# Three edits of instruction order in a one-core graph-attention kernel: the 26 products of a score block, the sums of the projection, and the first column maximum

## The chip, the cores and the metric

The kernel runs on one core of a Trainium2 chip. The metric is the device time of one launch in microseconds (us). A core has TensorE (PE, matrix products, which write PSUM banks), VectorE (DVE), ScalarE (ACT), GpSimd (POOL) and SyncE (SP, which here only issues DMAs). Each engine works off its own list of instructions in order, and an instruction may wait on semaphores that others raise.

## The reference

Two layers over N = 3327 nodes with D = 512 features. Layer 0 holds two rounds of graph attention, which take nearly all the time:

```python
for l in range(2):                       # W_stack[l] is 512 x 1024
    Wh, Ws = split(x @ W_stack[l], 2)    # projection
    scores = Wh @ Ws.T                   # 3327 x 3327
    a = softmax(scores, axis=-1) * adj
    x = leaky_relu(a @ Wh + x, 0.01)
x = layernorm(x0 + x)
# layer 1: sign(x) @ sign(weight).T, then adj @ (.), relu, residual, layernorm
```

## The kernel before

All matrix work of the attention is fp32, and fast matrix-multiplication schemes save products. Rows of the score matrix are handled in 13 pairs of 128-row tiles (q, the keys and values side) against 13 pairs of columns (g, the queries side); seven chunks c of four tiles group the pairs two by two (the last chunk has one pair only).

**Projection** (`project`, once per round). For every chunk, PE makes seven products for each half of the queries ("one" and "two", line 627) and, woven between them, seven for each pair of values (line 562). The seven products share three PSUM banks: product 3 ends bank Y, from which DVE adds a block (line 222, `b` and `wb`); product 7 extends bank Z, from which DVE adds the block called c22 (line 222, `gsp` and `wh`), and product 4, the last, may only be added onto Z when that has been read. At the same time DVE does, for this and the next chunk, the "turns": the sums `gsp` and `ge` of the queries just made (lines 244, 375), the transposes `xT` of the next chunk's rows (line 278), its key sums `s` and the sums `xt` of its right operand (line 244), and the sums `t` of the values. `weave` sorts several lists into one program order by a place between 0 and 1: an item of a plain list of n gets (i + 0.5) / n, and an item that is a pair carries its own place. POOL makes a further set of sums (`quad_sums`) and issues the stores. Sums live in a ring of slots, so that a sum may have to wait until the store of the slot's former owner has landed.

**Scores** (`scores`, `quad_scores`). The loop over steps v builds a list of (place, operation) for each step and sorts it by place. Work of a later step can be put in `early[v + n]`. In each round some blocks of four pairs, the quads (i = 1 to 4 in round 0, 1 to 3 in round 1), are made with 26 products (line 809) in the order of `ORDER`; 26 products take four steps, and product number n stands at (n + 0.5) / 6.5. They share three banks at a time. A product that goes to bank P, Q, R, S or T may start when the reader of the product before it in the same bank is done. A reader is an ACT copy (`keep_as`, line 815) 0.03 step after its product, a DVE addition (`out`, line 821) 0.082 step after it, or `seed`, an ACT copy back into bank Q (line 818). The other blocks use seven products (line 769) in banks Z, Y, X, with DVE additions at lines 905 and 911 and ACT copies at 891, 886, 915 and 919.

While chunk 0 is scored there are no attention products yet, so PE does the scores alone. From chunk 1 on, seven products of `values` (line 1100) are woven into each step, between the score products.

**Softmax**. The running maximum of each column (`maximum`, line 868) ends in `column_max`: fold and turn (lines 953 to 957), `across` (nine small operations, lines 964 to 969; on DVE for the first two pairs, copies on ACT for the others), `back` (line 974). For the first pair `spread` (ACT, line 1019) follows. Three steps before the values of a pair, DVE subtracts the maximum (`shift`, line 1024) and ACT takes the exponential (lines 1029, 1030); then DVE adds to the total (1035), masks (1040), counts (1063), and POOL sums (1053, 1073 to 1076).

Of the kernel before, what the change touches and what calls it, by code (L numbers as in the profile page):

```python
# [29 lines left out]

B11, T1, T2, B22, T3, B21, T4 = range(7)
QUADS = ((1, 2, 3, 4), (1, 2, 3))
ORDER = (11, 3, 8, 23, 16, 14, 12, 9, 22, 1, 20, 25, 4,
         13, 21, 7, 24, 6, 19, 15, 18, 5, 10, 17, 2, 0)
STAGED = ((11, 3, 23, 16, 12, 22, 9, 1, 25, 20, 8, 14, 4),
          (13, 7, 19, 6, 5, 18, 17, 15, 24, 10, 0, 21, 2))
EXTRA = (3, 23, 22, 9, 20, 21, 13, 7, 5, 2)
# [8 lines left out]
def kernel(  # L46
# [206 lines left out]
    def right_sums(b11, b12, b21, b22, t1, t2, t3, t4):  # L253
        return sums_by(
            nc.vector, (t1, b12, b11, ALU.subtract), (t2, b22, t1, ALU.subtract),
            (t3, b22, b12, ALU.subtract), (t4, b21, t2, ALU.subtract),
        )

    def run(todo):
        for do in todo:  # L260
# [202 lines left out]
    def project(l, pre):  # L463
# [36 lines left out]
        def transpose_x(c, a):  # L500
            turn_x(xTs[c], a, rows_of[c][a])
# [152 lines left out]
        chains, pairs_of, of_pair, more_of, rest = {}, {}, {}, {}, []  # L654

        def prepare(c):
            start, *chains[c] = queries(c, (ch_lane, ch_lane if c else acc_lane))
            return start
# [21 lines left out]
            weave(parts[0][1], parts[1][1], prepare(0))  # L680
            rest += parts[0][2] + parts[1][2]
        for c in range(NC):
            turns = list(rest)
            rest = more_of.pop(c, [])
            if c + 1 < NC:
                for a in range(len(tiles_of(c + 1))):
                    turns.append(lambda a=a: transpose_x(c + 1, a))
                transpose_x_begin(c + 1)
                pairs_of[c + 1] = [
                    project_values(c + 1, a, acc_lane)  # L690
                    for a in range(len(tiles_of(c + 1)) // 2)
                ]
                for part in pairs_of[c + 1]:
                    turns += part[0]
                turns += prepare(c + 1)
            if c + 2 < NC:
                load_x(c + 2)
            if c == 0:
                weave(*chains[c], turns)
            else:  # L700
                one, two = chains[c]
                pairs = pairs_of[c]
                quad, sums = [], []
                if c in QUADS[l]:
                    quad = quad_sums(l, c, of_pair[2 * c], of_pair[2 * c + 1])
                if len(pairs) == 2:
                    sums = [(0.53 + 0.09 * n, do) for n, do in enumerate(pairs[0][2])]
                rest = pairs[-1][2] + rest
                weave(one + two, sum((part[1] for part in pairs), []), turns, quad, sums)
# [11 lines left out]
    def attention(l, att):  # L721
# [6 lines left out]
        asum, ws, out_, early = {}, {}, {}, {}  # L728
# [45 lines left out]
        def quad_scores(c, i):  # L774

            mine = halves_of(c)
            w = len(mine) * P
            for q in (2 * i, 2 * i + 1):
                for g in mine:
                    sc[g, q] = slot([P, 2, HW], F32, f"s_{l}_{g}_{q}")  # L780
            lo, hi = mine[0], mine[-1]
            at = {}
            for e in range(4):
                q = 2 * i + e // 2
                at[f"c{e}0"] = sc[lo, q][:, e % 2, :w]
                at[f"c{e}1"] = sc[hi, q][:, e % 2, HW - w :]
            bank = {}

            def fresh(n):
                at[n] = att.tile([P, w], F32, tag=n, bufs=1, name=f"q{n}_{l}_{c}_{i}")  # L790
                return at[n]

            begins = {11: "P", 8: "Q", 3: "R", 24: "S", 10: "T", 17: "V"}
            joins = dict(zip(
                (23, 12, 1, 4, 7, 6, 18, 14, 22, 25, 21, 19, 5, 2, 16, 9, 20, 13, 15, 0),
                "PPPPPPPQQQQQQQRRRRST",
            ))

            def one(r):
                b = begins.get(r) or joins[r]  # L800
                if r in begins:
                    bank[b] = ps_ch.tile([P, w], F32, tag="ch", name=f"p{b}_{l}_{c}_{i}")
                if r in QUERY:
                    kind, k = QUERY[r]
                    right = query(c, kind)[:, k]
                else:
                    n = EXTRA.index(r)
                    right = query_extra(c, n // 2)[:, n % 2]
                nc.tensor.matmul(  # L809
                    bank[b], xs[c, i, f"x{r}"], right, start=r in begins, stop=True,  # L810
                    skip_group_check=True,
                )

            def keep_as(b, name):
                nc.scalar.copy(at[name] if name[0] == "c" else fresh(name), bank[b])  # L815

            def seed(b, name):
                nc.scalar.copy(bank[b], at[name])

            def out(name, b, other):  # L820
                nc.vector.tensor_tensor(at[name], bank[b], at[other], ALU.add)  # L821

            def more(name):
                nc.vector.tensor_tensor(at[name], at[name], at["u3"], ALU.add)

            place = {r: (n + 0.5) / 6.5 for n, r in enumerate(ORDER)}
            got = [(at_, lambda r=r: one(r)) for r, at_ in place.items()]
            for r, b, name in (
                (11, "P", "c10"), (8, "Q", "c21"), (23, "P", "c11"), (14, "Q", "c31"),
                (22, "Q", "u2"), (1, "P", "c30"), (25, "Q", "u3"), (20, "R", "c01"),  # L830
                (4, "P", "c20"), (13, "R", "c00"),
            ):
                got.append((place[r] + 0.03, lambda b=b, name=name: keep_as(b, name)))
            for r, b, name, other in (
                (16, "R", "c10", "c10"), (12, "P", "c31", "c31"), (9, "R", "c11", "c11"),
                (21, "Q", "c10", "c10"), (7, "P", "c00", "c00"), (24, "S", "u3", "u3"),
                (6, "P", "c01", "c01"), (5, "Q", "c01", "c01"), (15, "S", "c20", "c20"),
                (18, "P", "c21", "c21"), (2, "Q", "c11", "c11"), (10, "T", "c21", "c21"),
                (17, "V", "c30", "c30"), (0, "T", "c31", "c31"),
            ):  # L840
                got.append((
                    place[r] + 0.082, lambda name=name, b=b, other=other: out(name, b, other)
                ))
            got += [
                (place[21] + 0.09, lambda: seed("Q", "u2")),
                (place[6] + 0.05, lambda: more("c30")),
                (4.2, lambda: more("c00")),
            ]
            tops = [(g, q) for q in (2 * i, 2 * i + 1) for g in mine]
            for n, (g, q) in enumerate(tops):  # L850
                place_ = (4.75, 5.35, 5.75, 6.35)[n]
                got.append((place_, lambda g=g, q=q: maximum(g, q)))
            for at_, do in got:
                k = int(at_ // 1)
                early.setdefault(v + k, []).append((at_ - k, do))
# [14 lines left out]
        def scores(c, q, s):  # L870
# [50 lines left out]
            if s == 1:  # L921

                after.append((-0.05, lambda: maximum(mine[0], q)))
                if q == NQ - 1:

                    whole = column_max(mine[0])
                    if mine[0] == 0:
                        whole[2] = (0.97, whole[2][1])
                        early.setdefault(v + 2, []).append((-0.03, whole.pop()[1]))
                    after.extend(whole)  # L930
                    for i in mine[1:]:
                        for n, at, (_, do) in zip(
                            (2, 2, 3, 4), (0.68, 0.68, 0.97, 0.68), column_max(i)
                        ):
                            early.setdefault(v + n, []).append((at, do))
            if s == 0:
# [84 lines left out]
        def shift(g, q):  # L1021
            s = sc[g, q]
            at = beside[l][:, 0:1]
            nc.vector.tensor_tensor(s, s, at.to_broadcast([P, 2, HW]), ALU.subtract)  # L1024

        def exponential(g, q):
            if q == 0:
                total[g] = att.tile([P, 2, HW], F32, tag="total", name=f"total_{l}_{g}")
                nc.scalar.activation(total[g], sc[g, q], AF.Exp)
            nc.scalar.activation(sc[g, q], sc[g, q], AF.Exp)  # L1030
# [266 lines left out]
        for v in range(-LOOK - 4, len(steps)):  # L1297
# [24 lines left out]
                ]  # L1322
            if 0 <= v + 3 < len(steps):
                s3 = steps[v + 3]
                work += [(0.0, lambda: shift(*s3)), (0.12, lambda: exponential(*s3))]
                if s3[1] == NQ - 1 and s3[0] + 1 < NQ:
                    work.append((0.9, lambda: spread(s3[0] + 1)))
            if 0 <= v + 2 < len(steps):
# [359 lines left out]
```

## Time and profile before

| | |
|---|---|
| median of three runs | 2543.01 us (2541.51 to 2543.59) |
| the profiled execution, its own time | 2545.97 us |
| its span on the core | 2544.2 us |
| mean granted TensorE clock | 0.995 |
| PE, DVE, ACT, POOL busy | 98%, 80%, 33%, 57% |
| PE waits for DVE at line 821 (score blocks) | 14.6 us in 22 places |
| PE waits for DVE at line 222 (projection) | 11.2 us in 8 places |
| PE waits for DVE at line 911 (score blocks) | 8.0 us in 6 places |

The stages in us from the span's start: projection of round 0 up to 198, scores alone from there to 295, scores and values to 1233; projection of round 1 from there to 1406, scores alone to 1500, scores and values to 2437; then the last layer. A 128x256 fp32 product shows as two MATMUL records 0.216 us apart, so 0.432 us each. A row of the timeline gives start, duration, engine, line, operation, output and inputs, count, and in brackets the idle time of the engine before it with the engine that ended it. The page counts a wait of PE from the modelled end of the matmul before; the time that a wait costs, by the distance of starts over the usual 0.216 us, is about 0.17 us more.

### The profile page before, as it was taken

The page shows a single profiled execution, that of the slowest core. Times are in us where ns is not written, and L with a number is a line of the kernel's source. Part 1 is how long each engine was busy: PE and PEld are TensorE (multiplying, and loading weights), DVE is VectorE, ACT ScalarE, POOL GpSimd, SP SyncE. Part 2 cuts the span into 40 slices and gives each one's busy share as a digit, 9 for nine tenths or more (in the row PEclk, how much of TensorE's full clock was granted, in tenths as well). Part 3 has the DMA queues.
Part 4 walks back from the last instruction along what each step waited for, and adds up shares of the span by engine and source line. Part 5 has one row for each costly group of instructions (what it writes and reads, how often), then busy time and mean ns, then how long its engine had stood idle before and what let it go on. Part 6 is the DMA issues. An engine that isn't in the chain of part 4 may idle for free.

```text
span 2544.2 us, 39239 instructions
## 1 busy us (share of the span) xinstructions
PE 2490.9 (98%) x12056; PEld 2146.4 (84%) x12056; DVE 2046.2 (80%) x4097; ACT 841.5 (33%) x2094; POOL 1459.8 (57%) x2452
## 2 busy tenths in 40 slices
PE   9999999999999999999999999999999999999998
PEld 7887888888888888888878788888888888888886
DVE  6976787887878888778897778788787887878876
ACT  3323333333333243322232333332333323232234
POOL 3873456666666666545686345566555665555531
PEclk9999999999999999999999999999999999999999
DMA  6776767777677776897778676867868777688985
GB/s 197 267 284 225 268 218 267 250 252 268 228 269 248 254 258 232 271 316 266 237 254 298 237 272 230 277 239 261 273 225 276 247 266 260 229 281 287 315 277 175
DMA packets 313958, 652.17 MB, mean 256 GB/s; under 512 B 35373, under 2 KB 170661, under 8 KB 313742
## 3 DMA queue, kind: packets, MB, share of 16 engines
q1 hardware_dynamic: 279022, 539.75, 63.4%
q0 software_dynamic: 34720, 109.84, 11.5%
q8 instruction: 99, 1.62, 0.3%
q14 instruction: 117, 0.96, 0.1%
HBM read 539.15 MB, written 110.29 MB: 255 GB/s over the span
## 4 chain that ended last, share of the span: by engine, by line
PE 86%; DVE 8%; DMA 2%; issue 1%; POOL 1%; ACT 0%; SPq 0%; DVEq 0%; POOLq 0%; ACTq 0%
PE acc L1100 37%; PE pZ L769 10%; PE pP L809 6%; PE pQ L809 6%; PE pY L769 5%; PE pR L809 4%; PE agg L1416 3%; PE pX L769 2%; PE pZ_wh L562 2%; PE pZ_g L627 2%; PE pT L809 1%; PE pS L809 1%; PE pY_wh L562 1%; DVE s L821 1%; PE pm L455 1%
## 5 line engine op out<-in xcount | busy, mean ns | idle before, releaser
L1073 POOL TENSOR_TENSOR as<-s 128x128 f32<-128x128 f32 x338 | 204.6, 605 | 650.2 <-DVE s L1040 449.6
L1100 PE MATMUL acc<-ws,s 128*128 128x256 f32 x1352 | 402.3, 379 | 0.0
L1100 PE MATMUL acc<-ws,as 128*128 128x256 f32 x1352 | 376.4, 379 | 0.4 <-DMA ws<-ws_d 0.4
L1100 PE MATMUL acc<-wh,s 128*128 128x256 f32 x1352 | 376.3, 379 | 0.0
L1030 ACT ACTIVATE s<-s 128x512 f32<-128x512 f32 x338 | 213.3, 631 | 421.0 <-DVE s L1024 419.8
L1053 POOL TENSOR_TENSOR deg<-deg,adj 128x256 fp8e4<-128x256 fp8e4 x338 | 255.6, 756 | 55.3 <-DMA adj<-in_adjT_dram 40.5
L1100 PEld LDWEIGHTS acc<-ws,as 128*128 128x128 f32 x1352 | 249.4, 190 | 36.0 <-issue 3.3
L1100 PEld LDWEIGHTS acc<-wh,s 128*128 128x128 f32 x1352 | 250.6, 190 | 32.6
L1100 PEld LDWEIGHTS acc<-ws,s 128*128 128x128 f32 x1352 | 250.8, 190 | 30.8
L1035 DVE TENSOR_TENSOR total<-total,s 128x512 f32<-128x512 f32 x312 | 251.7, 807 | 0.0
L1040 DVE TENSOR_TENSOR s<-s,adj 128x512 f32<-128x512 f32 x338 | 241.3, 714 | 4.7 <-DMA adj<-in_adjT_dram 0.5
L1024 DVE TENSOR_TENSOR s<-s,beside 128x512 f32<-128x512 f32 x338 | 228.1, 675 | 16.2 <-ACT beside L1019 16.1
L868 DVE TENSOR_TENSOR top<-top,s 128x512 f32<-128x512 f32 x286 | 228.0, 799 | 16.1 <-ACT s L919 13.5
L769 PE MATMUL pZ<-ga,xs 128*128 128x256 f32 (+1 forms) x912 | 214.2, 359 | 9.0 <-DVE s L911 8.0
L1074 POOL TENSOR_TENSOR s<-s 128x128 f32<-128x128 f32 x338 | 199.8, 591 | 26.8
L1075 POOL TENSOR_TENSOR as<-s 128x128 f32<-128x128 f32 x338 | 189.9, 562 | 26.5
L1100 PE MATMUL acc<-wh,as 128*128 128x256 f32 x676 | 201.2, 379 | 0.0
L1076 POOL TENSOR_TENSOR as<-s,as 128x128 f32<-128x128 f32 x338 | 183.6, 543 | 26.4
L769 PEld LDWEIGHTS pZ<-ga,xs 128*128 128x128 f32 x912 | 165.1, 190 | 33.7 <-DVE s L911 10.4
L905 DVE TENSOR_TENSOR s<-pY,u 128x256 f32<-128x256 f32 (+1 forms) x84 | 33.8, 402 | 150.4 <-PE pY L769 138.2
L815 ACT COPY s<-pP 128x256 f32<-128x256 f32 (+1 forms) x196 | 70.2, 358 | 245.5 <-PE pP L809 197.5
L1100 PEld LDWEIGHTS acc<-wh,as 128*128 128x128 f32 x676 | 123.1, 190 | 19.1 <-issue 3.3
(266 smaller groups left out, 5086.7 us busy)
## 6 DMA issues: line engine op xcount, KB each, us to landing
ws<-ws_d SPq DMA_DIRECT2D x338, 512.0 KB
adj<-in_adjT_dram SPq DMA_DIRECT2D x351, 256.0 KB
xs<-xq_d SPq DMA_DIRECT2D x98, 832.0 KB
xs<-xs_d SPq DMA_DIRECT2D x84, 512.0 KB
xs<-xs_d SPq DMA_DIRECT2D x84, 384.0 KB
gs_d<-gsp POOLq DMA_DIRECT2D x84, 256.0 KB, 3.7
ge_d<-ge POOLq DMA_DIRECT2D x60, 256.0 KB, 3.2
ga<-gs_d SPq DMA_DIRECT2D x54, 256.0 KB
```

The source lines that it names most:

```text
L769: nc.tensor.matmul(ch[bank], xs[c, q, a][:, k], query(c, b)[:, k], start=(start and k == 0), stop=(k == 1), skip_group_check=True,)
L809: nc.tensor.matmul(bank[b], xs[c, i, f"x{r}"], right, start=r in begins, stop=True, skip_group_check=True,)
L868: nc.vector.tensor_tensor(top[i], top[i], t, ALU.max)
L1024: nc.vector.tensor_tensor(s, s, at.to_broadcast([P, 2, HW]), ALU.subtract)
L1030: nc.scalar.activation(sc[g, q], sc[g, q], AF.Exp)
L1035: nc.vector.tensor_tensor(total[g], total[g], sc[g, q], ALU.add)
L1040: nc.vector.tensor_tensor(s, s, adj[g, q], ALU.mult)
L1053: nc.gpsimd.tensor_tensor(deg[:, g], deg[:, g], adj[g, q][:, a], ALU.add, saturate=False)
L1073: nc.gpsimd.tensor_tensor(s3, a11, a21, ALU.subtract)
L1074: nc.gpsimd.tensor_tensor(a21, a21, a22, ALU.add)
L1075: nc.gpsimd.tensor_tensor(s2, a21, a11, ALU.subtract)
L1100: nc.tensor.matmul(acc[g][i // 2][:, i % 2], a[i], b[i], start=(q == 0 and i % 2 == 0), stop=(q == NQ - 1), skip_group_check=True,)
```

## The change

Three things move; no operation is added or taken away.

1. `ORDER`, the order of the 26 products of a quad, becomes another one. Readers move with their products. `more("c30")` is tied to product 15 in the place of product 6.
2. In `project` the turns get weights (0.5 for the sums of the chunk before and the key sums, 1.1 for a transpose, 0.7 for the sums `xt`), and `spaced` puts each at the middle of its weight's share of the total. Before, all turns lay at equal distances.
3. Of the first pair's column maximum, `across` and `back` go from places 0.97 of one step and -0.03 of the next to 0.16 and 0.17 of that next step, and the `shift` and exponential of the first step go from 0.0 and 0.12 to 0.19 and 0.31. For the second pair of each chunk `across` goes from 0.97 of the third step after to 0.2 of the fourth.

```diff
-ORDER = (11, 3, 8, 23, 16, 14, 12, 9, 22, 1, 20, 25, 4,
-         13, 21, 7, 24, 6, 19, 15, 18, 5, 10, 17, 2, 0)
+ORDER = (8, 11, 3, 14, 23, 16, 22, 12, 9, 25, 1, 20, 21,
+         4, 13, 7, 24, 19, 5, 15, 6, 2, 10, 18, 17, 0)
...
+    def spaced(todo):
+        ends = [0.0]
+        for w, _ in todo:
+            ends.append(ends[-1] + w)
+        return [
+            ((a + b) / 2 / ends[-1], do) for a, b, (_, do) in zip(ends, ends[1:], todo)
+        ]
+
+    def heavy(w, todo):
+        return [(w, do) for do in todo]
...
-            turns = list(rest)
+            turns = heavy(0.5, rest)
...
-                    turns.append(lambda a=a: transpose_x(c + 1, a))
+                    turns.append((1.1, lambda a=a: transpose_x(c + 1, a)))
...
-                    turns += part[0]
-                turns += prepare(c + 1)
+                    turns += heavy(0.5, part[0])
+                turns += heavy(0.7, prepare(c + 1))
+            turns = spaced(turns)
...
-                (place[6] + 0.05, lambda: more("c30")),
+                (place[15] + 0.05, lambda: more("c30")),
...
                     if mine[0] == 0:
-                        whole[2] = (0.97, whole[2][1])
-                        early.setdefault(v + 2, []).append((-0.03, whole.pop()[1]))
+                        early.setdefault(v + 2, []).extend(
+                            (at, whole.pop()[1]) for at in (0.17, 0.16)
+                        )
...
-                            (2, 2, 3, 4), (0.68, 0.68, 0.97, 0.68), column_max(i)
+                            (2, 2, 4, 4), (0.68, 0.68, 0.2, 0.68), column_max(i)
...
-                work += [(0.0, lambda: shift(*s3)), (0.12, lambda: exponential(*s3))]
+                at = 0.0 if any(s3) else 0.19
+                work += [(at, lambda: shift(*s3)), (at + 0.12, lambda: exponential(*s3))]
```

Per bank, the products of a quad keep their sequence. The distances, in products, that differ: 7 to 6 in bank P (2 before, 5 after), 4 to 7 in bank P (3 before, 2 after), 13 in bank R to 24, which starts bank S in the same place (3 before, 2 after), 21 to 19 in bank Q with the seed between (4 before, 5 after).

On DVE the projection's order changes so (chunk 3 of round 0): all four `gsp` sums and two `ge` sums now stand ahead of the first half's c22 addition, where only the first two `gsp` sums stood ahead of the Y addition; all ten `ge` sums and the first transpose stand ahead of the first sum `t`; and six key-sum operations in the place of five stand ahead of the second half's c22 addition. In round 0's chunk 4 and round 1's chunks 3 and 4 the number of key sums ahead of that addition stays six.

## The prediction

> **What bounds the kernel now.** I began with the page's first and fourth parts: which engine is busy, and of what the chain that ended last is made.
>
> ```profile
> PE 2490.9 (98%) x12056; PEld 2146.4 (84%) x12056; DVE 2046.2 (80%) x4097; ACT 841.5 (33%) x2094; POOL 1459.8 (57%) x2452
> ...
> PE 86%; DVE 8%; DMA 2%; issue 1%; POOL 1%; ACT 0%; SPq 0%; DVEq 0%; POOLq 0%; ACTq 0%
> ```
>
> PE sets the time; DVE's 8% of the chain are the moments at which PE waits for it. No product is added or removed, so only such moments can change. The view of the waits, for PE, says where:
>
> ```profile
> PE pP L809 <- DVE s L821: 14.6, 22, 2.0
> PE pZ_g L627 <- DVE gsp L222: 11.2, 8, 2.9
> PE pZ L769 <- DVE s L911: 8.0, 6, 2.5
> ```
>
> Columns: total, times, longest. I then read the timeline around the longest waits. The projection, PE and then DVE:
>
> ```profile
> 121.72 1.03 PE L562 MATMUL pX_wh<-wa,xT 128*128 128x256 f32 x4
> 125.64 2.07 PE L627 MATMUL pZ_g<-xt,m 128*128 128x256 f32 x4 [2.89 <-DVE gsp L222]
> 127.51 1.91 PE L562 MATMUL pZ_wh<-wsum,xT 128*128 128x256 f32 x4
> ```
> ```profile
> 106.45 0.42 DVE L222 TENSOR_TENSOR b<-pY_g,h_g 128x256 f32<-128x256 f32 x1 [0.29 <-PE pY_g L627]
> ...
> 115.36 0.57 DVE L244 TENSOR_TENSOR t<-wb,wh 128x256 f32<-128x256 f32 x1 [1.82 <-DMA gs_d<-gsp]
> ...
> 125.17 0.41 DVE L222 TENSOR_TENSOR gsp<-pZ_g,h_g 128x256 f32<-128x256 f32 x1
> ```
>
> Product 4 waits until DVE's c22 addition at 125.17 has read bank Z. DVE was 90% busy from 98 to 125 (24.22 of 27.00 us), yet stood idle 1.82 us at 115.36, because the first sum `t` needs a slot whose store had not landed. And four records of 1.03 us become four of 1.9 us: after the stall the granted clock is 0.50 (125.6 to 128.4) and 0.59 (128.4 to 132.4). So a stall can cost twice.
>
> The first column maximum:
>
> ```profile
> 282.92 0.45 DVE L974 STREAM_TRANSPOSE off<-mx 128x256 f32<-128x256 f32 x1
> 283.39 0.38 ACT L1019 COPY beside<-off 128x256 f32<-128x256 f32 x1 [2.85 <-DVE off L974]
> 283.80 0.69 DVE L1024 TENSOR_TENSOR s<-s,beside 128x512 f32<-128x512 f32 x1 [0.44 <-ACT beside L1019]
> 284.41 0.42 DVE L911 TENSOR_TENSOR s<-pZ,p 128x256 f32<-128x256 f32 x1
> 284.88 1.70 PE L769 MATMUL pZ<-ga,xs 128*128 128x256 f32 x4 [2.16 <-DVE s L911]
> 285.19 0.63 ACT L1030 ACTIVATE s<-s 128x512 f32<-128x512 f32 x1
> 286.62 0.37 ACT L919 COPY s<-pZ 128x256 f32<-128x256 f32 x1 [0.54 <-PE pZ L769]
> ```
>
> The addition of line 911 stands behind `across`, `back` and `shift`, PE behind it, and the clock is halved again. A quad while PE has scores alone:
>
> ```profile
> 253.39 0.95 DVE L868 TENSOR_TENSOR top<-top,s 128x512 f32<-128x512 f32 x1
> 254.26 0.41 DVE L821 TENSOR_TENSOR s<-pP,s 128x256 f32<-128x256 f32 x1
> 254.73 0.70 PE L809 MATMUL pP<-ga,xs 128*128 128x256 f32 x2 [0.85 <-DVE s L821]
> ```
>
> Product 6 follows 7 in bank P at two products' distance, and the reader of 7 stands behind a 0.95 us maximum. Costs below go by distances of starts over the usual pitch: this stall is 1.02.
>
> **Part 1, the projection.** Chunk ends now cost, in chunks 2, 3 and 4: round 0 1.96, 3.05 and 1.24 us, round 1 1.99, 3.09 and 0.41; 0.9 us more in three small ones (0.35, 0.39, 0.16). Behind each stall of 3 us, 14 records at 0.43 for 0.216 lose 2.9 to 3.0 more.
>
> DVE's idle time ahead of these additions, by the gaps in its timeline: round 0 chunk 2 1.13 + 0.44 + 0.72; chunk 3 0.7 + 1.8; round 1 chunk 2 1.14 + 0.44 + 0.75, chunk 3 2.3. After the change, `gsp` sums, `ge` sums and the first transpose stand there ahead of `t` and have their inputs, so they fill much of it; their own places later come free, and the c22 addition moves forward. Against that, one more key sum (a 0.41 to 0.53 us row, spaced 0.4) stands ahead of the second half's addition in chunk 3 of round 0. Chunk 3: 3.05 - 2.5 + 0.45 = 1.0 if only the second half gains nothing more; placing operations one by one with their durations I get 0.6, and 0.8, 0.1 for chunks 2 and 4. Round 1: 0.8, 0.7, and 1.0 for chunk 4, where DVE's 2.23 us idle at 1350.13 is a load that no order hastens. Stalls of 1.96, 1.99 and 2.15 us (98.31, 1306.53, 1699.84) left the clock alone, so both slow stretches go. Sum: round 0 -1.16 - 2.45 - 2.9 - 1.14 = -7.7; round 1 -1.19 - 2.39 - 3.0 + 0.6 = -6.0. I take 12 of the 13.7, since the transposes wait for loads that POOL and SP issue in their own order (`xT` waited for one until 1353.7). Ends: all stalls gone, 1.96 + 3.05 + 1.24 + 1.99 + 3.09 + 0.41 + 0.9 + 5.9 = 18.5 gained; no idle time filled and a key sum added in four chunks, 2 lost.
>
> **Part 2, the order of 26.** No instruction is added. Two regimes.
>
> c = 0, PE alone (seven quads, 0.43 us per product). Product 6 stalls now: 1.02 five times, 0.32 twice, 5.7 in all. At distance 5 this is gone. Late next is product 7, at distance 2 behind 4 instead of 3; and bank P was made free there by a copy, while bank Q's chain is longer: 21's DVE addition, ACT's `seed`, the next product's copy, all ahead of the copy of 4 on ACT. End of 21 to start of 7: 0.63 + 0.42 + 0.04 + 0.27 + 0.37 + 0.05 = 1.78, against 1.3 that three products give: 0.5 each. Product 20, behind a maximum in five quads: 0.3 each. So 7 x 0.5 + 5 x 0.3 = 5.0, net -0.7. The first quad's wait for its load (0.70 at 213.92, 1.36 at 1420.38) meets a product one place later: -0.43 twice. The bank R stall of 0.72 at 1443.33 likewise: -0.4. Together -2.0. Ends: -9 (no stall left in these quads) and +3 (0.43, one more product's time, seven times).
>
> c from 1 on (42 quads; `values` products lie between, 0.865 us per product). Product 6 stalls five times, all in round 1, i = 2 (0.66, 0.77, 0.77, 0.65, 1.85), where residual work and a maximum delay DVE. There product 7 stalls instead, its chain 0.2 longer, the worst one 0.75: 6.3 for 4.7, +1.6. Product 18 stalls six times (0.91, 0.33, 2.15, 1.23, 0.77, 0.62: 6.0); its predecessor's reader comes one product earlier relative to it, which leaves 2.15 - 0.865 = 1.3, 0.4 and 0.05, 1.9 with some rounding up: -4.1. In the other 37 quads I find 0.5 to 1.2 us between the seed chain's end and product 7, hence nothing. Net -2.5. Ends: -11 (all go) and +5 (a further 0.12 in each quad, a quarter of the 0.5 found at c = 0).
>
> **Part 3, the column maximum.** First pair: the addition of line 911 now runs at once, 281.90. `across` to `shift` took 283.80 - 281.43 = 2.37 us, and starts at 282.24: `shift` at 284.61. What queues behind this on ACT: `spread`, two exponentials, and then the copies of lines 915 and 919. The exponentials start at 285.33 and 285.98, the copies at 286.52 and 286.8, and the next block's product, whose bank the last copy reads, at 287.2. Without a stall it would start at 284.29 (284.88 - 2.32, plus four records of 0.43): 2.9 lost. Before, 2.32 and 2.67 (1491.49) were lost here, so +0.6 and +0.2. DVE lets PE go; ACT stops it.
>
> The clock: stalls of 3.05 and 3.09 cost 2.9 to 3.0 more, that of 2.32 cost 1.5 (seven records), that of 2.67 none (granted clock 1.00 from 1491 to 1494). 2.9 is nearest to the 3 us rows: 2.9 each, 5.8 less 1.5 = +4.3. Second pair: `across` out of the way at 0.2, the stalls of 1.41 at 294.12 and 1499.05 go: -2.8. Part 3: 0.8 + 4.3 - 2.8 = +2.3. Ends: -9.3 (all of it gone: 5.0 + 1.5 + 2.8) and +5.1 (second pair gains nothing).
>
> The Trainium skill's page "TensorE: Matmul & The Clock Gate", Part 1, speaks of a free-running window of 3413 ns in which PE must be idle before its clock is halved, and advises against idle gaps above about 3 us. By that alone no stall of 2.32 us should have halved anything, yet the trace shows it at 284.88; by the page part 3 would be 4.3 us cheaper and the time that much lower. The same page has ACT and DVE as strict FIFO: it speaks against this part, since copies of ACT that are ready cannot pass exponentials that are not.
>
> **Sum.** -12 - 2.0 - 2.5 + 2.3 = -14.2. The profiled execution took 2545.97 us, its span 2544.2 and 1.8 around it; 2545.97 - 14.2 = 2531.8. It lies 3.0 above the median of 2543.01, so I forecast 2528.8 us for the median.
>
> **Rivals.** A measurement of this kernel tells about 0.2%, 5.1 us, from no change.
>
> *The projection stays with DVE.* For: 90% busy there, and the `t` sums' slots still come free when stores land, up to 115.26 in chunk 3. Then stalls shrink by about 1 us each in four chunks, the 3 us ones stay above 2, and one of the slow stretches stays: -4 for -12, 2537.
>
> *Spacing does nothing at all.* `t` waits for the same store, and DVE idles elsewhere: +2 for -12, with the rest 2543, no change.
>
> *Slower: the seed chain.* Product 7 at distance 2 waits in every quad, not in five. It takes a 21 whose DVE addition is late by the 0.5 to 1.2 us of slack and more, for instance behind a maximum or a mask. Against: only round 1's i = 2 shows such lateness now. For: the new order shifts all readers. At 0.5 us per quad, 42 quads cost 21: 2550. From 14.2/42 = 0.34 us per quad on it outweighs all the gains.
>
> *Better: the new ACT wait is short.* If the first pair's stall stays under 2.2 us, the clock stays up: part 3 is -2.8 - 1.5 - 0.6 for +2.3, and with a projection at -13 the time is 2521.
>
> **How the numbers follow.** Forecast 0.45, by itself 2522 to 2536; better 0.18; projection half 0.15; nothing from spacing 0.08; seed chain 0.14. Range 2516 to 2543: it leaves out the seed chain and the far ends of the best case. Faster by over 5.1 us (below 2537.9): 0.45 + 0.18 + two thirds of 0.15 = 0.73; within: 0.05 + 0.08 = 0.13; slower 0.14.
>
> **What will show it.** PE's waits for `gsp` at line 222: from 11.2 us to about 4, no granted clock of 0.5 near 126 and 1334. Waits of PE at product 18 gone save two or three; product 6 replaced by product 7, with an ACT copy as releaser. At 284 to 288 PE waits for ACT's copy (line 919 before, 931 now), with halved clock behind it; at 294 and 1499 no wait. I am wrong if product 7 waits outside round 1's i = 2, if line 222's sum stays above 8, or if the first pair shows no ACT wait.

## The result and the profile after

The changed kernel is slower: 2555.25 us (2552.61 to 2556.02, five runs) against 2543.59 us, ratio 1.0045 with a 95% interval of 1.0031 to 1.0060. The forecast was 2528.8 us, range 2516 to 2543. The profiled execution took 2555.67 us, its span 2553.9; before it was 2545.97 and 2544.2.

The page, part 1 and the first line of part 4, of the kernel after:

```profile
PE 2491.3 (98%) x12056; PEld 2145.2 (84%) x12056; DVE 2051.6 (80%) x4097; ACT 833.4 (33%) x2094; POOL 1460.5 (57%) x2452
...
PE 35%; DVE 4%; issue 1%; ACT 1%; POOL 0%; DVEq 0%; ACTq 0%; POOLq 0%
```

PE works as long as before, so again only its waits have changed. (The chain of part 4 covers only 41% of the span this time, so its shares can't be set against those before.) The view of waits, PE's rows, of the kernel after (total, times, longest):

```profile
PE pP L821 <- ACT s L827: 23.3, 24, 1.8
PE pQ L821 <- DMA xs<-xq_d: 6.7, 5, 2.1
PE pZ_g L638 <- DVE gsp L222: 5.4, 9, 1.0
PE pY_g L638 <- ACT gsp L235: 4.2, 1, 4.2
PE pY L781 <- ACT s L931: 3.9, 2, 2.2
```

Read against the view before, the change did what it says: of the three DVE releasers only line 222 is left in the first rows. It fell from 11.2 to 5.4 us with none above 1.0; line 911 (923 now) left the first rows. But ACT, which released almost nothing before, now holds PE for 23.3 + 4.2 + 3.9 us, and a load for 6.7. Each stage taken from its first product on (before: 193.1, 295.1, 1233.0, 1400.6 and 1500.0 us), the time moved so (change of a stage's length in the two profiled executions, after minus before; the execution before had the clock halved behind both 3 us stalls of its projections and lay 2.4 us above its median):

| stage | round 0 | round 1 |
|---|---|---|
| projection | -5.3 | +2.6 |
| scores alone | +0.6 | -0.6 |
| scores and values | +4.7 | +8.1 |

So the loss lies mainly in "scores and values", where the forecast had -2.5 us, and the projection's gain in round 0 is half undone in round 1. Of 24 waits in the first row, twelve are of product 7. The other twelve are of product 23, once in each first quad (i = 1) of the chunks from 1 on: 0.89 to 1.94 us each by distances of starts, 16.6 us together. No step of the forecast speaks of product 23.

The timeline of the kernel after around one of them, ACT, DVE and PE rows picked out:

```profile
442.39 0.40 ACT L982 COPY mx<-mx 32x8 f32<-32x8 f32 x2
442.81 0.37 ACT L1139 COPY op<-acc 128x256 f32<-128x256 f32 x1
...
443.22 0.42 DVE L1140 TENSOR_TENSOR h<-acc,op 128x256 f32<-128x256 f32 x1 [1.07 <-ACT op L1139]
...
448.58 0.68 DVE L1037 TENSOR_TENSOR s<-s,beside 128x512 f32<-128x512 f32 x1
...
449.29 0.63 ACT L1043 ACTIVATE s<-s 128x512 f32<-128x512 f32 x1 [2.52 <-DVE s L1037]
449.83 0.35 ACT L827 COPY s<-pP 128x256 f32<-128x256 f32 x1
...
450.23 0.70 PE L821 MATMUL pP<-gb,xs 128*128 128x256 f32 x2 [0.91 <-ACT s L827]
```

The same place before, where the quad's first product starts at 450.20 (in the kernel after at 445.71):

```profile
446.09 0.37 ACT L1126 COPY op<-acc 128x256 f32<-128x256 f32 x1 [0.23 <-PE acc L1100]
446.49 0.42 DVE L1127 TENSOR_TENSOR h<-acc,op 128x256 f32<-128x256 f32 x1 [0.24 <-ACT op L1126]
...
450.89 0.37 ACT L815 COPY s<-pP 128x256 f32<-128x256 f32 x1 [1.41 <-PE pP L809]
...
451.95 0.68 DVE L1024 TENSOR_TENSOR s<-s,beside 128x512 f32<-128x512 f32 x1
...
452.66 0.63 ACT L1030 ACTIVATE s<-s 128x512 f32<-128x512 f32 x1 [1.40 <-DVE s L1024]
```

Two edits meet here. In the new `ORDER` product 11 is the second product and not the first, so its ACT copy (`s<-pP`) moved from place 0.11 to 0.26, past the exponential at 0.12: before it ran 1.77 us ahead of the exponential, now behind. And `across` of the second pair, at 0.2 of the fourth step, put its ACT copies (line 982) ahead of the copy `op` (ACT's copy of an attention product, which DVE adds to the output sum `h`): `op` starts 2.9 us ahead of the quad's first product in place of 4.1, DVE's `h` is late by as much, and so are the sums and the maximum behind it, `shift` (2.87 after the first product in place of 1.75) and the exponential. Product 11's copy waits for all of that, and product 23 for the copy.

### The profile page after: what moved, and what is told of

Its sections match the earlier page's. It is cut to its first block, busy times and chain, and to the rows that moved or that the text cites. A ratio compares the mean times of both kernels' runs of the same rounds, so it can differ in the third digit from the quotient of the medians.

```text
span 2553.9 us, 39256 instructions
## 1 busy us (share of the span) xinstructions
PE 2491.3 (98%) x12056; PEld 2145.2 (84%) x12056; DVE 2051.6 (80%) x4097; ACT 833.4 (33%) x2094; POOL 1460.5 (57%) x2452
## 5 line engine op out<-in xcount | busy, mean ns | idle before, releaser
L880 DVE TENSOR_TENSOR top<-top,s 128x512 f32<-128x512 f32 x286 | 233.7, 819 | 16.1 <-ACT s L931 13.5
L1087 POOL TENSOR_TENSOR s<-s 128x128 f32<-128x128 f32 x338 | 194.3, 575 | 26.8
L1069 POOL DMA_DIRECT2D adj_d<-ab x169 | 94.4, 559 | 62.7 <-ACT ab L1061 35.0
```

What stands on the lines that cost most here:

```text
L880: nc.vector.tensor_tensor(top[i], top[i], t, ALU.max)
L1087: nc.gpsimd.tensor_tensor(a21, a21, a22, ALU.add)
```

## The experiments

Times are medians; "before" was 2543.9 to 2544.8 us beside these runs. Ratios are to the kernel before with 95% intervals; differences to the changed kernel are to its 2555.25 us, taken beside a kernel before of 2543.59.

**e1, the order alone.** The diff's `ORDER` and `more("c30")`, applied to the kernel before.

> The kernel before with the new ORDER (and its more) alone. Theory: the order costs time because product 11, moved from the first to the second place, has its ACT copy behind the exponential at 0.12, so product 23 waits in each first quad of the chunks from 1 on (12 stalls, 16.6 us in the changed kernel), against about 5 us won at products 6 and 18: slower by 10 to 14 us, near 2555. Rival, the order is good and the loss lies in the projection and the column maximum: faster by 3 to 6 us, near 2539.

2545.29 us, ratio 1.0005 (0.9995 to 1.0014). Neither theory: alone, the order changes nothing that can be measured. Product 23's twelve stalls are six of 0.33 to 0.52 here. That the forecast's 4.5 us did not come is seen in the waits inside the quads, which (those over 0.25 us) add to 23.6 us by starts against 23.4 before: gone are those of products 6 (10.4), 18 (6.0) and 13 (2.4), and in their place stand product 7 with 11.6 (the forecast had 9.8), product 21 with 3.8, most of it for loads, product 23 with 2.3 and products 2 and 10 with 1.8. The forecast had no term for products 23, 2 and 10.

**e2, the spacing alone.** The weights, `spaced` and `heavy`, applied to the kernel before.

> The kernel before with the weights and spacing of the projection alone. Theory: round 0 gains 5 to 6 us; round 1 gives back what it gains at line 222 to one wait of 4.4 us of the ACT copy of c21 in chunk 4, whose ring slot now has another former owner, and to the halved clock behind it (2.7 us), net +3: near 2541, faster by 2 to 3 us. Rival, that stall comes from DMA traffic of this one execution: then it is missing here and the time is 2534, faster by 9 us.

2545.23 us, ratio 1.0005 (0.9995 to 1.0014). The wait for the slot (of `c21`, the block that ACT copies from bank Z after product 4) is there again (4.5 us), so it isn't of one execution; the gain expected over it did not show in the median.

**e3, the column maximum alone.** Both pairs' new places applied to the kernel before.

> The kernel before with the column maximum's new places alone. Theory (DVE lets PE go, ACT stops it): the stalls of 2.3 and 2.7 us at line 911's readers become stalls of about 2 us at the next block's product with halved clock in both rounds, the second pair's 1.4 us go twice: between 3 us faster and 1 us slower, near 2542.5. Rival, the ACT wait is new cost with nothing gained: 4 us slower or more.

2548.08 us, ratio 1.0016 (1.0007 to 1.0026): the rival's number, though not its reason. Its two halves are taken apart below (e15, e16).

**e4, the exponential behind the copy.**

```diff
-                work += [(at, lambda: shift(*s3)), (at + 0.12, lambda: exponential(*s3))]
+                till = 0.28 if c > 0 and i == 4 else at + 0.12
+                work += [(at, lambda: shift(*s3)), (till, lambda: exponential(*s3))]
```

> The changed kernel with the exponential of one step per chunk (the one in which the first quad starts, chunks 1 to 6) put at place 0.28 in the place of 0.12, just behind the ACT copy of product 11. Theory: the stalls of product 23 go, 12 of 1.06 to 1.94 us: faster than the changed kernel by 14 to 17 us, near 2540. Rival, the copy is late by itself (product 11 or bank P are late, or the exponential's delay moves the stall to the sums and masks behind it): less than 4 us gained, 2551 or more.

2541.23 us, 14.0 less than the changed kernel, ratio 0.9988 (0.9978 to 0.9998). All twelve stalls of product 23 are gone. Timeline of e4 at the same place (first product at 441.31):

```profile
442.86 0.37 ACT L827 COPY s<-pP 128x256 f32<-128x256 f32 x1 [0.49 <-PE pP L821]
...
444.77 0.59 PE L821 MATMUL pP<-gb,xs 128*128 128x256 f32 x2
...
444.89 0.63 ACT L1043 ACTIVATE s<-s 128x512 f32<-128x512 f32 x1 [1.66 <-DVE s L1037]
```

The copy runs 2 us ahead of the exponential, and product 23 (444.77) waits for nothing. The exponential itself lost no time: it starts 3.58 us after the first product, as in the changed kernel.

**e5, `across` put back.**

```diff
-                            (2, 2, 4, 4), (0.68, 0.68, 0.2, 0.68), column_max(i)
+                            (2, 2, 3, 4), (0.68, 0.68, 0.97, 0.68), column_max(i)
```

> The changed kernel with the second pair's across put back to 0.97 of the third step. Theory (two edits meet): across at 0.2 stands ahead of ACT's copy op, which holds DVE's output sums, maximum and shift 1.1 us later, and with them the exponential behind which product 11's copy waits; put back, the stalls of product 23 fall from 16.6 us to about 2.5, the two of 1.4 us at the second pair return: faster than the changed kernel by 10 to 13 us, near 2543. Rival, the order alone makes them: no more than 2 us gained, 2553 or more.

2543.7 us, 11.6 less than the changed kernel, ratio 1.0000 (0.9990 to 1.0009). Product 23's stalls are 2.6 us. With e1 and e3 this fills the square: order without `across` 2.3 to 2.6 us of stalls at 23, both 16.6, `across` without the new order none at 23. It takes both.

**e6, another owner for the slot.**

```diff
-            turns = spaced(turns)
+            turns = spaced([(1, do) for _, do in turns] if (l, c) == (1, 4) else turns)
```

> The changed kernel with equal weights in one chunk, the turns of chunk 4 of round 1. The ring then gives c21's tile of that chunk a slot whose former store was issued far earlier. Theory: the stall of 4.4 us and the halved clock behind it (2.7 us) go, a wait at line 222 of 0.4 to 2.3 us comes back: faster than the changed kernel by 4 to 7 us, near 2550. Rival, the stores of that time are late for whoever needs a slot, and DVE's or ACT's next owner stops PE as long: less than 2 us gained.

2553.12 us, 2.1 less than the changed kernel, which is not clear of noise (ratio 1.0042, 1.0027 to 1.0056, against 1.0045): the rival, as far as this can tell. The wait in the kernel after, and what took its place in e6 (timelines):

```profile
1352.44 0.37 ACT L235 COPY gsp<-pZ_g 128x256 f32<-128x256 f32 x1 [6.83 <-DMA ws_d<-t]
1352.87 2.07 PE L638 MATMUL pY_g<-xt,msum 128*128 128x256 f32 x4 [4.21 <-ACT gsp L235]
```
```profile
1351.76 0.37 ACT L219 COPY h_g<-pY_g 128x256 f32<-128x256 f32 x1 [5.93 <-DMA ws_d<-t]
1352.18 1.22 PE L638 MATMUL pY_g<-xT,msum 128*128 128x256 f32 x2 [3.30 <-ACT h_g L219]
```

c21's copy got a free slot; the next copy that needs one (`h_g`) stands before a store of the same kind. In both kernels ACT goes on at about 1352, when a `ws_d` store of `t` lands.

**e7, the first exponential behind ACT's copies.**

```diff
-                work += [(at, lambda: shift(*s3)), (at + 0.12, lambda: exponential(*s3))]
+                work += [(at, lambda: shift(*s3)), (0.12 if any(s3) else 0.72, lambda: exponential(*s3))]
```

> The changed kernel with the first step's exponential at 0.72 in the place of 0.31, behind ACT's copies of lines 927 and 931. Theory: the next block's product no longer waits for the copy (2.4 and 1.9 us) and the clock stays up (1.7 us each): faster than the changed kernel by 5 to 8 us, near 2548. Rival, the loads of that time are late too (0.4 and 1.0 us before the same products) and take the place of the wait, or a later wait for the exponential appears: less than 3 us gained.

2551.34 us, 3.9 less than the changed kernel, between theory and rival (ratio 1.0033, 1.0019 to 1.0047; the interval overlaps that of the changed kernel). The waits for the copy fell from 2.4 and 1.9 us (by starts) to 0.9 and none; a load and a second copy behind it took 0.4 to 1.3 us.

**e8, three repairs.** e4, e6 and e7 together, and `across` at 0.2 for the second pair of chunk 0 only (`if i == 1`).

> The changed kernel with the three repairs together: exponential at 0.28 in the step of the first quad, across at 0.2 for the second pair of chunk 0 only, equal weights in chunk 4 of round 1, first exponential at 0.72. Theory: the gains add, 14 + 6 + 6 off 2555: near 2529, faster than the kernel before by 12 to 16 us. Rival, the waits are replaced by others behind them: 2538 or more.

2535.49 us, ratio 0.9961 (0.9945 to 0.9977): faster than both kernels. It is 19.8 us below the changed kernel, and e4, e6 and e7 gained 14.0 + 2.1 + 3.9 = 20.0: the repairs seem to add up, and two of them were expected to be worth more. The fourth edit, `across`, was not run by itself on top of e4, so the sum takes it as worth nothing there.

**e9, the seed chain.**

```diff
-                (place[21] + 0.09, lambda: seed("Q", "u2")),
+                (place[4] + 0.04, lambda: seed("Q", "u2")),
```

> The changed kernel with the seed at 0.04 step behind product 4 in the place of 0.09 behind product 21, that is behind ACT's copy of 4 in the place of ahead of it. Theory (seed chain): product 7, at distance 2 behind 4, no longer waits for 21's DVE addition; its 12 stalls (3.9 us while PE has scores alone, 6.7 us in round 1, i = 2) go but for 1 to 2 us: faster than the changed kernel by 6 to 9 us, near 2548. Rival, distance 2 is too short by itself, or DVE's lateness stops the next product (24 or 19) instead: less than 4 us gained.

2555.86 us: nothing gained, the rival. PE's waits in e9:

```profile
PE pP L821 <- ACT s L827: 14.4, 12, 1.8
PE pQ L821 <- DMA xs<-xq_d: 8.4, 6, 3.1
PE pS L821 <- ACT s L827: 5.9, 7, 2.4
```

Product 7's twelve waits are gone (the twelve that are left are product 23's). But in round 1, i = 2, product 24 now waits, for the copy of 13, which now stands behind the late seed and an exponential: 6.4 us by starts for the 6.7 before. While PE has scores alone the 3.9 us at product 7 did go. What took them back is product 24 in the other quads: laid start by start against the kernel after, the two having one order of PE's products, product 7 wins 10.9 us over all 49 quads and product 24 loses 12.1, in places of 0.2 to 0.3 us besides those of i = 2. (This profiled execution, the slowest of the five at 2560.39, also has one wait for a load of 3.2 us at 1092.91 with the clock at 0.57 behind it.)

**e10, five repairs.** e8, the seed of e9, and in `STAGED` (which half of a quad's left operands is loaded first) products 21 and 4 exchanged, with ACT's copies of them in `quad_sums`.

> The three repairs with two more: the seed as in the run before, and product 21's left operand loaded with a quad's first half and product 4's with the second (the new ORDER starts 21 at place 12, where the load of the first half ended before). Theory: 7 us from product 7 and 2 to 4 us from product 21's waits for loads off 2535.5: near 2525, faster than the kernel before by 16 to 21 us. Rival, waits replaced by others: 2532 or more.

2531.65 us, ratio 0.9952 (0.9938 to 0.9966): 3.8 less than e8, not the 10 expected. No run takes its two additions apart; e9 gained nothing by the seed alone, while the waits of product 21 (7.8 us by starts in e8) became waits of 1.8 at product 4.

**e11, the repairs with the old order.** e8 with the old `ORDER` and `more`.

> The three repairs with the old ORDER. Theory: the new order without seed and load repairs is worth about 4 us (products 6, 18, 11 and 13 stall 22 us in the old one, 7, 20, 21 and 8 some 18 in the new): near 2538, slower than the three repairs with the new order by 1 to 5 us, and by 10 or more than the five repairs. Rival, the order is worth nothing or costs: 2534 or less.

2538.91 us, ratio 0.9981 (0.9972 to 0.9990): 3.4 more than e8 (all eleven runs lie above all five of e8) and 7.3 more than e10 (the intervals lie apart). With its collisions removed the new order pays.

**e12, spacing in round 0 only.** e10 with `spaced([(1, do) for _, do in turns] if l == 1 else turns)`.

> The five repairs with equal weights in all of round 1, spacing in round 0 only. Theory: in round 1 the slots' stores stop PE in one way or the other, so that the spacing there is worth 1 to 4 us only: near 2527, slower than the five repairs by that. Rival, spacing is worth as much as in round 0 (5 to 6 us), 2531 or more; or less than nothing there, 2524 or less.

2530.84 us, ratio 0.9953 (0.9939 to 0.9967): the fastest, not distinguishable from e10, which has equal weights in round 1's chunk 4 already. In the rest of round 1 the spacing is worth nothing that can be measured.

**e13 and e14, the spacing in one round each,** on the kernel before (equal weights where `l == 1`, then where `l == 0`).

> The kernel before with the spacing in round 0 only. Theory: round 0 wins the stalls at line 222 (about 4 us; the halved clock behind the 3 us stall is a matter of chance, so it adds 1 to 2 us on average and not 2.9): faster by 3 to 6 us, near 2540. Rival, the first quads then wait for loads that come no earlier and give it back: within 2 us of the kernel before.

> The kernel before with the spacing in round 1 only. Theory: the wait of ACT's copy for its slot (4.4 to 5 us, with halved clock at times) takes what line 222 gives: between 2 us faster and 3 us slower. Rival, round 1 is where spacing alone loses everything that round 0 wins: 4 us slower or more.

e13: 2540.83 us, ratio 0.9983 (0.9975 to 0.9992), 3.4 faster. e14: 2547.97 us, 1.0012 (1.0003 to 1.0021), 3.7 slower; its profile has the same wait for `gsp` at line 235, 4.2 us. Together they are e2: a gain in round 0, the same lost in round 1.

**e15 and e16, the halves of the column maximum,** on the kernel before: the second pair's `across` alone, then the first pair alone.

> The kernel before with the second pair's across at 0.2 of the fourth step alone. Theory: it takes the two stalls of 1.4 us (2.8 us) and holds DVE's output sums back by 1.1 us in each chunk from 1 on, where the product that fills beside then waits (0.3 to 1.0 us in 11 places): slower by 1 to 4 us, near 2546. Rival, without the new order there is enough slack in each chunk: 2 to 3 us faster.

> The kernel before with the first pair's edit alone. Theory: one wait for another, 1.2 to 1.9 us at the next product and 1.0 to 1.6 at a load for 2.3 to 2.7 at line 911: within 2 us of the kernel before. Rival, it is this half that costs the 4 us: 3 us slower or more.

e15: 2547.63 us, 1.0015 (1.0006 to 1.0024). e16: 2542.42 us, 0.9996 (0.9986 to 1.0005). e3's cost lies in `across`. In e15's profile "scores and values" is 2.9 and 3.5 us longer than before, and PE waits where it never did (e15, waits):

```profile
PE beside L1151 <- DVE s L1024: 1.6, 2, 0.8
...
PE pQ L809 <- ACT s L815: 0.7, 1, 0.7
```

The product that fills `beside` comes once per chunk, behind the late `shift`. The second row is product 14 of a first quad (1502.42), behind ACT's copy of product 8. So even without the new order the delay reaches PE. Laid start by start against the kernel before, `beside` accounts for 1.0 of the 2.9 us and 2.0 of the 3.5, product 14 for 0.8 and 2.2 (in e3: 1.0 and 2.0, 0.7 and 2.2); what is left in round 0 falls on products 9 and 11. No run isolates one of them.

## Why the prediction was wrong

Sum against measurement (medians, us):

| term | forecast | measured alone |
|---|---|---|
| projection | -12, from round 0 -7.7 and round 1 -6.0 | +1.2 (e2); round 0 -3.4, round 1 +3.7 (e13, e14) |
| order of 26 | -4.5 | +1.3 (e1) |
| column maximum | +2.3; first pair +5.1, second -2.8 | +4.0 (e3); first pair -1.8, second +3.4 (e16, e15) |
| the parts together | none | about +5: 11.7 slower against 6.5, by e1, e2 and e3; about +8 for `across` alone, 11.6 by e5 against 3.4 by e15 |

**The step that failed first** is in part 2: "In the other 37 quads I find 0.5 to 1.2 us between the seed chain's end and product 7, hence nothing." That is right for product 7 (outside round 1's i = 2 it does not stall from chunk 1 on) and was taken as right for the quad. Every reader moved, and only the chain with the shortest distance was followed. Product 11's copy kept its distance of three products to 23, yet changed its neighbours in ACT's queue. In the changed kernel product 23 waited 16.6 us for that copy in twelve places, and e4, which puts the exponential behind the copy, won 14.0 back. A distance in products says nothing of what stands between on the reader's engine. The forecast used just this argument in part 3 (copies behind exponentials) and did not carry it to part 2.

**The second step** is in part 3: "Second pair: `across` out of the way at 0.2, the stalls of 1.41 at 294.12 and 1499.05 go: -2.8.", with no price at the other end. The 2.8 were won (both stalls are gone). But `across` has ACT copies from the third pair on, and what is queued behind them in the fourth step is `op`, the first link of DVE's output sums. It was priced at chunk 0, where there are no output sums, and it runs in every chunk. Measured alone the second pair cost 3.4 us. The first pair missed the other way, at -1.8 (not told from nothing) for +5.1: its term of 4.3 for the clock took two slow stretches of 2.9 as certain. That the whole of part 3, +4.0 for +2.3, comes near is luck.

**The projection** had its mechanism right and the sum wrong. Stalls at line 222 in round 0 were put at 0.8, 0.6 and 0.1 us; they came as 0.82, 0.80 and 0.89. Two terms were off. The slow stretches: 5.9 us of gain for two of them, read from one execution that had both in full. They are a matter of chance (last section), and cost about half of that on average. And round 1, where the stalls at line 222 were put at 0.8, 0.7 and 1.0 us: they came as 0.34, 1.17 and none, with three more of 0.60, 0.82 and 1.04 (1268.19, 1281.20, 1319.04), and one of 4.37 by starts for a slot. The 1.0 us for chunk 4 stood for a load, but with operations issued in another order the ring hands out other slots. The slot of c21's copy now belongs to a `t` whose store was issued at 1344 and landed at 1352. The forecast says that waits for slots gate DVE's sums; it did not ask which copies on ACT take slots too. e6 shows that this owner alone is not to blame: with another one the next copy stands before a store of the same kind, issued at 1342.65 and landed at 1351.66.

**Loads of a quad.** "The first quad's wait for its load ... meets a product one place later: -0.43 twice" had the sign wrong: product 21 is in the second half's load and moved to place 12, while place 13 was the first to need that half before. The forecast also read the two waits as one load's: the view puts that at 213.92 down to ACT's copy and that at 1420.38 to the load `gb<-ge_d` of the queries' sums, and product 21 waits for `xs<-xq_d`. The waits of product 13 (0.70, 1.35, and 0.39 at 1093.58) became waits of product 21 of 1.75 and 1.09, with 1.74 at 1092.74 and 0.65 at 2317.07 besides. With product 21 loaded in the first half (e10) product 4 is the first to need the second, at place 13 as before, and 1.2 and 0.6 us are left.

**What held.** Product 7 in round 1, i = 2: 6.7 us for 6.3. At c = 0: 0.58 for 0.5. Product 18 no longer stalls, but not for the reason given: it stands three products behind 6, its predecessor in bank P, in both orders. Before, at 1699.84, it waited for 6's addition (DVE, 1699.37), which stood behind the residual's work and `more("c30")`. In the new order 6 comes three places later and its addition (1706.25) with it, and it is product 2 that stalls at this place, 0.40 us. The first pair: PE waits for ACT's copy and not for DVE's addition, 2.4 and 1.9 us for 2.9, with the clock halved behind both (granted 0.51 from 283.6 to 286.6 and 0.50 from 1495 to 1498). None of the three signs by which the forecast said it would be wrong appeared (product 7's waits in chunk 0 were forecast): they watched the waits that it knew of, and the loss came at others. The rival "seed chain" had the right sign and about the right time, 2550, with the wrong mechanism: product 7 does not wait in every quad, and from chunk 1 on only where the forecast had it. Its reasoning, "the new order shifts all readers", was the right one, followed to the wrong reader.

## What to carry to other kernels

When an instruction is given another place, list for every engine that it touches what now stands ahead of it, and for the slowest of these what feeds it; the distance to its next user is only half of the matter. Price two moves together wherever their operations share an in-order queue: here the order alone cost nothing that can be measured (1.0005) and the column maximum alone 1.0016, while all together cost 1.0045. And a stall's side effects read from a single profile, such as a slow clock, are worth their average over several profiles, not what that one shows.

## What the runs showed of the hardware

The same stall halves PE's clock in some executions and not in others. Windows right behind the stall of chunk 3 (span; busy time and count of PE, PEld, DVE, ACT and POOL; granted clock; DMA share; GB/s): the kernel before, behind 3.05 and 3.09 us,

```profile
125.60:132.00 6.40, 6.36 (x16) 5.11 (x17) 6.33 (x14) 1.10 (x3) 2.76 (x6) 0.52 0.80 309
1333.90:1340.50 6.60, 6.60 (x17) 5.30 (x18) 6.50 (x14) 1.10 (x3) 6.29 (x11) 0.54 0.77 273
```

e1, behind 3.08 and 3.06 us,

```profile
125.90:132.40 6.50, 6.41 (x30) 5.66 (x31) 6.43 (x15) 2.26 (x7) 2.82 (x7) 1.00 0.80 311
1328.30:1335.00 6.70, 6.66 (x23) 5.58 (x24) 6.60 (x14) 1.80 (x5) 6.39 (x11) 0.75 0.76 271
```

and e3, behind 2.89 and 3.07 us:

```profile
125.50:132.00 6.50, 6.43 (x22) 5.42 (x23) 6.43 (x15) 1.58 (x5) 2.83 (x6) 0.74 0.79 307
1332.00:1338.60 6.60, 6.57 (x30) 5.81 (x31) 6.50 (x14) 2.42 (x7) 6.29 (x11) 1.00 0.76 272
```

Clocks of 0.52, 0.54, 1.00, 0.75, 0.74 and 1.00 behind nearly equal stalls; a stall of 2.32 us also cost seven slow records in one place (281.11 in e1) and none in another (1487.83). At 1.00 such a window holds 30 of PE's records; two hold 13 or 14 fewer, two 7 or 8 fewer and two none fewer, a mean of 7 at 0.216 us: about 1.5 us per stall and not the 2.9 that the forecast took off for each.

The Trainium skill, "TensorE: Matmul & The Clock Gate", Part 1, calls the window in which PE's activity is judged free-running, so that the point of change varies: these rows agree with that. Its length of 3413 ns as the idle time needed does not fit the 2.32 us at 281.11, nor the 1.85 us at 1495.04 in the kernel after.
